# Softmax sums over all eight key blocks on GpSimd, the rotation's sums on VectorE, a part of the output division on ScalarE

## The chip, the cores and the metric

The kernel runs on one core of one Trainium2 chip. The metric is the device time of a run in microseconds (us). The kernel before was timed three times; a profile of one further execution was taken. In this text PE is TensorE, DVE is VectorE, ACT is ScalarE, POOL is GpSimd, and SP is the queue that issues every DMA of this kernel.

## The reference

The input x has 4 batches of 1024 rows of 128 numbers. Three layers follow one another, each added to x: a mixture of 8 experts with a soft routing (half its output is added), an attention with 16 heads, and the same mixture again. The attention is

```
h = layernorm(x) * ln_scale + ln_bias
c_q, c_kv = h @ w_down_q.T, h @ w_down_kv.T              # 64 latents each
q, k, v = (c_q @ w_up_q.T), (c_kv @ w_up_k.T), (c_kv @ w_up_v.T)   # 16 heads of 64
q, k = rope(q), rope(k)      # e*cos - o*sin and e*sin + o*cos for the even and odd elements
attn = softmax(q k^T / 8)    # 1024 keys for each query
out  = (attn @ v) @ w_out.T + residual
```

All data are 32-bit floats. In the layers around it the attention is added to x once more.

## The kernel before

**Stages.** The first mixture takes about the first 230 us (`ffn`), the attention stands from about 250 to 1525 us, and the second mixture (`ffn2`) ends the kernel. Preparation of later stages (layer norms, projections to the latents, routing weights) runs in small steps in the background of the stage before, as generators: `attn_pre` and `ffn_pre`.

**Units, slots and groups.** Heads are taken in pairs, of which one lies on partitions 0 to 63 and the other on 64 to 127. A unit U is half a head pair: 512 queries of two heads against all 1024 keys. There are 64 units, 16 for each batch. The keys of a unit are taken in 8 blocks of 128, and one block of one unit is a slot. Four slots make a group, so a unit lasts two groups; there are 128 groups. The attention's main loop runs over the groups.

**A slot.** `score` (L734) computes the transposed scores of 128 keys by 512 queries in four matmuls for each of the two heads (L746); the last of the four subtracts the row maxima. ACT takes the exponential from PSUM into the tile `p` (L750), 1024 wide for both heads; there are 8 buffers of `p`. `values` (L764) multiplies `p` by the latents of its keys into the PSUM bank `psc` (L769). It runs one group later. PSUM has 8 banks: five rotate among the scores (psS0 to psS3 and psX), two take the maxima (psA), one the values (psC).

**Maxima.** `passA` (L709) runs 15 slots ahead and computes the same scores the other way round, one matmul (L720) for each head into psA0 or psA1, of which VectorE takes the maximum (L721). Eight such pairs of matmul and maximum belong to each group, spread between its score matmuls.

**Softmax sums.** `accumulate` (L754) adds up the blocks of `p` on GpSimd into `acc` (L762), 1024 wide. The constant `DIRECT = 1` says how many of the 8 blocks are left out of it. So GpSimd makes six additions for a unit, of blocks 0 to 6, and block 7 stands by itself. At the end of the group that follows the unit's two, `den` (L773) sums over the 128 keys on PE with a matrix of ones (L781): eight matmul records over `p` of block 7, eight over `acc`. ACT copies the sums out (L783), and two small DMAs on SP turn them into `dT`, a column for each 128 queries (L787, L789). One group later `outp` (L792) multiplies the unit's values by the output weights (L802) into psX for one head and psS3 for the other, as `bankO` says. Its inner function `add` takes the reciprocal of `dT` (L809) and, for each of the two heads and four row blocks, multiplies by it and adds to the residual X (L813), 128 wide, on VectorE.

**Rotation.** `rope` (L602) works in stages for one half of a head group, in attention every second (even) group. "fetch" reads latents, "mm" gives six matmuls (L624) to the group, even elements into psX and odd ones into psS3. "o" and "e" multiply each by two tables, 1024 wide, on VectorE into the SBUF tile `rt` (L631). "sum" adds the two halves of `rt` on GpSimd into the tile `eo` (L634), 1024 wide. A group later ACT rounds `eo` to a high part (L639, "hi0" and "hi1") and GpSimd computes the low part (L647, "lo"); the stages "dhi" and "dlo" store them by DMA. The first nine rotations run before the attention loop through `attn_first`, with the stages "o", "e" and "sum"; 55 run inside it.

**Order.** Every engine runs its instructions in the order in which this program gives them, and each SP DMA waits in that queue as well. In a group the loop gives: the score matmuls of both heads with the maxima between them, then matmuls of `outp` (odd groups) or of the rotation (even groups); one step of the preparation; `den` (even groups); the rotation's VectorE and GpSimd work; `add` of `outp` (odd groups); the casts; and the values of the group before, with another preparation step between them. `step(most, vector)` picks a generator whose next step is of a kind up to `most`: OTHER, VECTOR (VectorE work) or PE (matmuls or transposes and what reads them); with `vector` false, VECTOR steps are left out. Another `step(OTHER)` stands in the middle of the group's rows. The variables `hurry` and `late` steer these calls.

Of the kernel before, what the change touches and what calls it, by code (L numbers as in the profile page):

```python
# [10 lines left out]
F32 = mybir.dt.float32  # L11
F32R = mybir.dt.float32r
AF = mybir.ActivationFunctionType
ALU = mybir.AluOpType
# [4 lines left out]
B, S, D = 4, 1024, 128  # L19
# [3 lines left out]
TPB = S // 128  # L23
# [4 lines left out]
AHEAD = 15  # L28
NSLOT = B * 128
NGRP = NSLOT // 4  # L30
DIRECT = 1
PBUFS = 8
MAXIMA = ((3, 8, 13), (0, 5, 10))
OTHER, VECTOR, PE, NEVER = 0, 1, 2, 3
NROPE = 9
# [6 lines left out]
class Kernel:  # L42
# [559 lines left out]
    def rope(self, n, stage):  # L602


        nc, P = self.nc, self.prep
        w = self.rope_of.setdefault(n, {})
        b, m = divmod(n, 16)
        g, qk, h = m // 4, m // 2 % 2, m % 2
        scr = (self.k_scr if qk else self.q_scr)[b][g]
        cs = slice(512 * h, 512 * h + 512)  # L610

        if stage == "fetch":
            assert (b, h) in self.latents
            w["C"] = P.tile([128, 2, 512], F32R, name="C_l", bufs=2)
            for r in (0, 64):
                self.dma(out=w["C"][r:r + 64], in_=self.c_scr[b][h][64 - 64 * qk:128 - 64 * qk])
        elif stage == "mm":
            ps = w["ps"] = self.rope_banks
            hi, lo = w["C"][:, 0, :], w["C"][:, 1, :]

            def mm(k, eo):
                wt, c = ((self.wup1, hi), (self.wup1, lo), (self.wup2, hi))[k]
                r64 = slice(64 * eo, 64 * eo + 64)
                nc.tensor.matmul(ps[eo], wt[r64, qk * 4 + g, :], c[r64, :], start=k == 0, stop=k == 2)  # L624

            for eo in range(2):
                self.halves[eo] += [lambda k=k, eo=eo: mm(k, eo) for k in range(3)]
        elif stage in ("o", "e"):
            k = "eo".index(stage)
            ps = w["ps"][k].unsqueeze(1).to_broadcast([128, 2, 512])  # L630
            nc.vector.tensor_tensor(self.rt[:, 2 * k:2 * k + 2, :], ps, self.table[:, 1 - k:3 - k, cs], ALU.mult)  # L631
        elif stage == "sum":
            w["eo"] = P.tile([128, 2, 512], F32, name="eo", bufs=2)
            nc.gpsimd.tensor_tensor(w["eo"], self.rt[:, 0:2, :], self.rt[:, 2:4, :], ALU.add)  # L634
        elif stage in ("hi0", "hi1"):
            k = int(stage[2])
            if k == 0:
                w["hi"] = P.tile([128, 2, 512], F32R, name="hi_r")
            nc.scalar.copy(w["hi"][:, k, :], w["eo"][:, k, :])  # L639
        elif stage == "dhi":  # L640
            self.dma(out=scr[0:2, :, :, cs].rearrange("s h i t -> (h i) s t"), in_=w["hi"])
        elif stage in ("lo0", "lo1"):
            k = int(stage[2])
            eo = w["eo"][:, k, :]
            nc.gpsimd.tensor_tensor(eo.bitcast(F32R), eo, self.f(w["hi"][:, k, :]), ALU.subtract)  # L645
        elif stage == "lo":
            nc.gpsimd.tensor_tensor(w["eo"].bitcast(F32R), w["eo"], self.f(w["hi"]), ALU.subtract)  # L647
        elif stage == "dlo":
            self.dma(out=scr[2:4, :, :, cs].rearrange("s h i t -> (h i) s t"), in_=w["eo"])
            self.roped.add((b, g, qk, h))  # L650
            del self.rope_of[n]
# [140 lines left out]
    def outp(self, U, osb, dT):  # L792


        nc = self.nc
        P, half = divmod(U, 2)
        b, j = divmod(P, 8)
        po = self.bankO or self.psA

        def mm(i, hh):  # L800
            r = slice(64 * hh, 64 * hh + 64)
            nc.tensor.matmul(po[hh][:, i * 128:(i + 1) * 128], osb[r, i * 128:(i + 1) * 128], self.G[r, j, :], start=True, stop=True)  # L802

        for hh in range(2):
            self.halves[hh] += [lambda i=i, hh=hh: mm(i, hh) for i in range(4)]

        def add():
            rT = self.ms.tile([128, 8], F32, name="rT")
            nc.vector.reciprocal(rT, dT)  # L809
            for hh in (1, 0):  # L810
                for i in range(4):
                    x = self.X[:, b * TPB + 4 * half + i, :]
                    nc.vector.scalar_tensor_tensor(x, po[hh][:, i * 128:(i + 1) * 128], rT[:, 4 * hh + i:4 * hh + i + 1], x, ALU.mult, ALU.add)  # L813

        self.at(self.group, add)

    def run(self):
        nc, tc = self.nc, self.tc
# [104 lines left out]
        a, c, e = (NP - 3) % 3, (NP - 2) % 3, (NP - 1) % 3  # L923
# [15 lines left out]
        def step(most, vector=True):  # L939


            turns["next"] += 1
            found = []
            for i in range(2):
                k = 1 + (turns["next"] + i) % 2
                while streams[k] and streams[k][0] not in needs:
                    v = next(streams[k][0], self)
                    if v is self:
                        streams[k].pop(0)
                    else:  # L950
                        needs[streams[k][0]] = v or OTHER
                if streams[k] and need(k) <= most:
                    found.append(k)
            found = [k for k in found if vector or need(k) != VECTOR]
            if found:
                k = max(found, key=need)
                gen = streams[k][0]
                kind = need(k)
                v = next(gen, self)
                if v is self:  # L960
                    streams[k].pop(0)
                else:
                    needs[gen] = v or OTHER
                return kind
            return OTHER


        ROPE = {"mid": {2: "dhi"}, "side": {0: "mm"}, "end": {-1: "fetch", 0: "o e sum", 2: "dlo"}, "cast": {1: "hi0 hi1 lo"}}

        def rope(g, place):  # L970
            for d, stages in ROPE[place].items():
# [5 lines left out]
        for g in range(NGRP + 1):  # L977
            s0 = 4 * g
            self.group, self.slot = g, s0
            rope(g, "side")  # L980
            self.run_later(g, "side")

            def rows(hh):
                maxima = lambda i: self.passA(s0 + AHEAD + i, hh) if s0 + AHEAD + i < NSLOT else None
                for n in range(16):
                    if n in MAXIMA[hh]:
                        yield lambda n=n: maxima(MAXIMA[hh].index(n))
                    yield lambda n=n: self.score(s0 + n // 4, hh, n % 4) if g < NGRP else None  # L990
                if hh == 1:
                    yield lambda: maxima(3)
                yield from side[hh]
                if hh == 0:
                    yield lambda: maxima(3)

            side = self.halves
            for n, pair in enumerate(zip_longest(rows(0), rows(1))):
                for fn in pair:
                    if fn:  # L1000
                        fn()
                if n == 9:
                    rope(g, "mid")
                    self.run_later(g, "mid")
                    step(OTHER)
            self.halves = [[], []]

            b, i = divmod(s0, 128)
            if i == 8 and 1 <= b < B:
                streams[1].append(pre2(b - 1))  # L1010
            self.nrest = 0
            hurry = g < 16 or g >= NGRP - 8
            late = step(PE, hurry) == PE or g % 2 == 0 or hurry or g >= 88
            if g and g % 2 == 0:
                self.den(g // 2 - 1)
            rope(g, "end")
            self.run_later(g, "end")
            if g == 1 or (g < NGRP and g % 4 == 3):
                P = g // 4 + 3 if g > 1 else 2
                if P < NP:  # L1020
                    for n, fn in enumerate(self.loads(P)):
                        self.at(g + 1 + n // 8, fn, ("mid", "end")[n // 4 % 2])
                if P == NP + 1:
                    self.ffn_weights2(self.QT[a], self.KT[a], self.QT[c])
                    self.dma(out=xs[0], in_=self.x2_scr[0])

            rope(g, "cast")
            for s in range(s0 - 4, s0):
                if s >= 0:
                    self.values(s)  # L1030
                if s == s0 - 3:
                    step(VECTOR, late)
        for i in range(2):
            for k in range(2):
                for hl in range(2):
                    c = slice(512 * k, 512 * k + 512)
# [3 lines left out]
        with ExitStack() as ctx:  # L1040
# [5 lines left out]
            g = self.ffn_pre(self.prep, (6, 7), x_of, self.wts2[:, 3].rearrange("p e t -> p t e"), rows=3)  # L1046
# [65 lines left out]
```

## Time and profile before

| | us |
|---|---|
| median of 3 runs | 1679.14 |
| lowest, highest | 1677.74, 1685.03 |
| the profiled execution's own time | 1681.56 |
| its span, first to last instruction | 1679.8 |
| PE busy in the span | 1620.7 |
| GpSimd busy | 1467.3 |
| VectorE busy | 1272.5 |
| ScalarE busy | 932.9 |
| mean granted TensorE clock | 0.990 |

The page of a profile gives the busy time and its share of the span for each engine, and then the span in 40 slices of 42 us with the busy share of each in tenths. A group line reads: source line, engine, operation, tile written <- tiles read, shapes, count, then the busy time in us and the mean duration in ns, then how long the engine stood idle just before these instructions and who ended that. Two figures of one instruction kind must be kept apart: its duration, and the distance from one start to the next when several follow one another, which is often shorter, since the end of one overlaps the start of the next. A timeline line gives start, length, engine, line and count. Matmuls overlap, so PE's busy time is that of the union.

### The profile page before, as it was taken

The page shows a single profiled execution, that of the slowest core. Times are in us where ns is not written, and L with a number is a line of the kernel's source. Part 1 is how long each engine was busy: PE and PEld are TensorE (multiplying, and loading weights), DVE is VectorE, ACT ScalarE, POOL GpSimd, SP SyncE. Part 2 cuts the span into 40 slices and gives each one's busy share as a digit, 9 for nine tenths or more (in the row PEclk, how much of TensorE's full clock was granted, in tenths as well). Part 3 has the DMA queues.
Part 4 walks back from the last instruction along what each step waited for, and adds up shares of the span by engine and source line. Part 5 has one row for each costly group of instructions (what it writes and reads, how often), then busy time and mean ns, then how long its engine had stood idle before and what let it go on. Part 6 is the DMA issues. An engine that isn't in the chain of part 4 may idle for free.

```text
span 1679.8 us, 31615 instructions
## 1 busy us (share of the span) xinstructions
PE 1620.7 (96%) x11412; PEld 1055.3 (63%) x11412; DVE 1272.5 (76%) x2456; ACT 932.9 (56%) x1964; POOL 1467.3 (87%) x821
## 2 busy tenths in 40 slices
PE   7897989999999999999999999999999999999998
PEld 5786665566656566665656566665666655656776
DVE  5674667878878778787778888887887877835887
ACT  4674565655565555655555555555555554555554
POOL 5658779999999999998999999999999987786676
PEclk9998999999999999999999999999999999999999
DMA  7024647555555555555555555555556632034443
GB/s 222 1 62 131 172 126 168 142 140 145 128 127 140 135 143 141 127 139 139 127 139 127 139 143 137 127 140 139 142 131 146 137 93 64 2 90 128 141 136 99
DMA packets 241148, 212.30 MB, mean 126 GB/s; under 512 B 157664, under 2 KB 170592, under 8 KB 240224
## 3 DMA queue, kind: packets, MB, share of 16 engines
q1 hardware_dynamic: 240992, 210.28, 49.5%
q8 instruction: 90, 1.47, 0.4%
q14 instruction: 66, 0.54, 0.1%
HBM read 130.39 MB, written 79.82 MB: 125 GB/s over the span
## 4 chain that ended last, share of the span: by engine, by line
PE 75%; POOL 7%; DVE 4%; ACT 3%; issue 3%; DMA 1%; SPq 1%; DVEq 0%; POOLq 0%; ACTq 0%
PE psc L769 23%; PE ps_s L746 22%; PE ps_a L720 6%; POOL acc L762 4%; PE ps_s L781 3%; PE ps_s L498 3%; PE psx L746 3%; PE ps_s L418 3%; PE psx L453 2%; PE psx L802 2%; PE psx L624 1%; PE ps_s L802 1%; ACT p L750 1%; PE psc L389 1%; SPq L51 1%
## 5 line engine op out<-in xcount | busy, mean ns | idle before, releaser
L721 DVE TENSOR_REDUCE m<-ps_a 128x1 f32<-128x512 f32 x1024 | 685.2, 690 | 231.9 <-PE ps_a L720 190.0
L762 POOL TENSOR_TENSOR acc<-acc,p 128x1024 f32<-128x1024 f32 x320 | 761.1, 2378 | 33.2 <-ACT p L750 13.7
L750 ACT ACTIVATE p<-ps_s 128x512 f32<-128x512 f32 x896 | 478.5, 602 | 308.4 <-PE ps_s L746 298.0
L746 PE MATMUL ps_s<-QT,KT 64*128 64x512 f32 x2688 | 551.3, 398 | 1.4 <-DVE rt L631 0.6
L769 PE MATMUL psc<-p,ckn 128*64 128x512 f32 x2048 | 467.7, 598 | 0.0
L746 PEld LDWEIGHTS ps_s<-QT,KT 64*128 64x128 f32 x2688 | 352.2, 185 | 138.1 <-issue 93.3
L720 PE MATMUL ps_a<-KT,QT 64*128 64x512 f32 x1024 | 420.3, 421 | 11.1 <-DVE m L721 8.3
L769 PEld LDWEIGHTS psc<-p,ckn 128*64 128x64 f32 x2048 | 135.6, 136 | 255.8 <-issue 249.8
L746 PE MATMUL ps_s<-maxr,one_row 64*128 64x512 f32 x896 | 238.4, 392 | 0.0
L720 PEld LDWEIGHTS ps_a<-KT,QT 64*128 64x128 f32 x1024 | 185.2, 185 | 43.2 <-DVE m L721 17.6
L762 POOL TENSOR_TENSOR acc<-p 128x1024 f32<-128x1024 f32 x64 | 152.9, 2388 | 42.4 <-ACT p L750 42.2
L634 POOL TENSOR_TENSOR eo<-rt 128x1024 f32<-128x1024 f32 x64 | 153.9, 2405 | 2.0 <-DMA qs<-eo 1.9
L771 ACT COPY osb<-psc 128x512 f32<-128x512 f32 x64 | 37.6, 588 | 195.5 <-PE psc L769 195.5
L647 POOL TENSOR_TENSOR eo<-eo,hi_r 128x1024 fp32r<-128x1024 f32 x55 | 132.0, 2401 | 0.0
L746 PEld LDWEIGHTS ps_s<-maxr,one_row 64*128 64x128 f32 x896 | 123.2, 185 | 13.3
L402 POOL TENSOR_TENSOR X<-X,dtmp 128x512 f32<-128x512 f32 x54 | 69.2, 1282 | 57.6 <-ACT dtmp L401 49.4
L746 PE MATMUL psx<-QT,KT 64*128 64x512 f32 x384 | 111.0, 394 | 0.0
L506 POOL TENSOR_TENSOR p<-eo,p 128x512 fp32r<-128x512 f32 x42 | 64.0, 1531 | 35.0 <-ACT p L505 27.4
L639 ACT CAST hi_r<-eo 128x512 fp32r<-128x512 f32 x128 | 73.9, 626 | 23.4 <-POOL eo L645 21.6
L813 DVE SCALAR_TENSOR_TENSOR X<-ps_s,rT,X 128x128 f32<-128x128 f32 x252 | 71.1, 344 | 15.4 <-PE ps_s L802 8.2
L750 ACT ACTIVATE p<-psx 128x512 f32<-128x512 f32 x128 | 77.0, 602 | 4.9 <-ACT p L750 1.8
L746 PEld LDWEIGHTS psx<-QT,KT 64*128 64x128 f32 x384 | 71.2, 186 | 7.3
(219 smaller groups left out, 2355.6 us busy)
## 6 DMA issues: line engine op xcount, KB each, us to landing
C_l<-cs SPq DMA_DIRECT2D x128, 256.0 KB
QT<-qs SPq DMA_DIRECT2D x256, 128.0 KB
KT<-ks SPq DMA_DIRECT2D x256, 128.0 KB
qs<-hi_r SPq DMA_DIRECT2D x32, 512.0 KB
qs<-eo SPq DMA_DIRECT2D x32, 512.0 KB
ks<-hi_r SPq DMA_DIRECT2D x32, 512.0 KB
ks<-eo SPq DMA_DIRECT2D x32, 512.0 KB
rt<-wt SPq DMA_DIRECT2D x52, 256.0 KB
```

What stands on the lines that cost most here:

```text
L402: nc.gpsimd.tensor_tensor(X[:, t:t + 4, :], X[:, t:t + 4, :], tmp, ALU.add)
L506: (nc.gpsimd if m < N - 1 else nc.vector).tensor_tensor(sh[:, 1, :], hp, self.f(sh[:, 0, :]), ALU.subtract)
L634: nc.gpsimd.tensor_tensor(w["eo"], self.rt[:, 0:2, :], self.rt[:, 2:4, :], ALU.add)
L639: nc.scalar.copy(w["hi"][:, k, :], w["eo"][:, k, :])
L647: nc.gpsimd.tensor_tensor(w["eo"].bitcast(F32R), w["eo"], self.f(w["hi"]), ALU.subtract)
L720: nc.tensor.matmul(self.psA[hh], self.QT[P % 3][r, 0, q0:q0 + 128], self.KT[P % 3][r, 0, kk * 512:kk * 512 + 512], start=True, stop=True)
L721: nc.vector.tensor_reduce(m[0][:, hh, qb, kk:kk + 1], self.psA[hh], AX.X, ALU.max)
L746: nc.tensor.matmul(ps, w, x, start=k == 0, stop=k == 3)
L750: nc.scalar.activation(self.p_of[s][:, hh, :], ps, AF.Exp, scale=0.125)
L762: nc.gpsimd.tensor_tensor(acc, self.p_of[s - 1] if c == 1 else acc, self.p_of[s], ALU.add)
L769: nc.tensor.matmul(self.psC[64 * hh:64 * hh + 64, :], self.ckn[b % 2][:, c, :], self.p_of[s][:, hh, :], start=c == 0, stop=c == 7)
L813: nc.vector.scalar_tensor_tensor(x, po[hh][:, i * 128:(i + 1) * 128], rT[:, 4 * hh + i:4 * hh + i + 1], x, ALU.mult, ALU.add)
```

## The change

`DIRECT` becomes 0: GpSimd adds block 7 to `acc` too, as a seventh addition, and `den` multiplies only `acc` by the ones.

The rotation inside attention gets one stage, "vector", for "o e sum". VectorE multiplies the even elements by two tables into `rt`, as "e" did; it multiplies the odd elements by each of the two tables into the PSUM banks of the even and the odd elements, in place; and it adds each bank to a half of `rt`, into `eo`. The stages "o", "e" and "sum" stay for the nine first rotations.

In `add`, ScalarE multiplies the first head's four blocks by the reciprocals, in their PSUM bank. VectorE multiplies and adds the second head's four blocks as before, and then adds the whole first bank, 512 wide, to X.

The loop's preparation steps are steered by a new variable, `free`, true in groups below 16, in odd groups, and from group 112 on. Where it is false, only steps of the kind OTHER are taken.

```diff
-DIRECT = 1
+DIRECT = 0
...
+        elif stage == "vector":
+            w["eo"] = P.tile([128, 2, 512], F32, name="eo", bufs=2)
+            (even, odd), rt = w["ps"], self.rt
+            nc.vector.tensor_tensor(rt[:, 0:2, :], even.unsqueeze(1).to_broadcast([128, 2, 512]), self.table[:, 1:3, cs], ALU.mult)
+            nc.vector.tensor_tensor(even, odd, self.table[:, 0, cs], ALU.mult)
+            nc.vector.tensor_tensor(odd, odd, self.table[:, 1, cs], ALU.mult)
+            nc.vector.tensor_tensor(w["eo"][:, 1, :], odd, rt[:, 1, :], ALU.add)
+            nc.vector.tensor_tensor(w["eo"][:, 0, :], even, rt[:, 0, :], ALU.add)
...
-            for hh in (1, 0):
-                for i in range(4):
-                    x = self.X[:, b * TPB + 4 * half + i, :]
-                    nc.vector.scalar_tensor_tensor(x, po[hh][:, i * 128:(i + 1) * 128], rT[:, 4 * hh + i:4 * hh + i + 1], x, ALU.mult, ALU.add)
+            t0 = b * TPB + 4 * half
+            for i in range(4):
+                c = slice(i * 128, (i + 1) * 128)
+                nc.scalar.activation(po[0][:, c], po[0][:, c], AF.Identity, scale=rT[:, i:i + 1])
+            for i in range(4):
+                x = self.X[:, t0 + i, :]
+                nc.vector.scalar_tensor_tensor(x, po[1][:, i * 128:(i + 1) * 128], rT[:, 4 + i:5 + i], x, ALU.mult, ALU.add)
+            x = self.X[:, t0:t0 + 4, :]
+            nc.vector.tensor_tensor(x, po[0].rearrange("p (t d) -> p t d", t=4), x, ALU.add)
...
-        ROPE = {"mid": {2: "dhi"}, "side": {0: "mm"}, "end": {-1: "fetch", 0: "o e sum", 2: "dlo"}, "cast": {1: "hi0 hi1 lo"}}
+        ROPE = {"mid": {2: "dhi"}, "side": {0: "mm"}, "end": {-1: "fetch", 0: "vector", 2: "dlo"}, "cast": {1: "hi0 hi1 lo"}}
...
-            hurry = g < 16 or g >= NGRP - 8
-            late = step(PE, hurry) == PE or g % 2 == 0 or hurry or g >= 88
+            free = g < 16 or g % 2 == 1 or g >= 2 * (16 * B - NROPE) + 2
+            step(PE if free else OTHER, free)
...
-                    step(VECTOR, late)
+                    step(VECTOR, free)
```

## The prediction

> **What bounds the kernel now.** I read the page first: busy shares, then the 40 slices.
>
> ```profile
> PE 1620.7 (96%) x11412; PEld 1055.3 (63%) x11412; DVE 1272.5 (76%) x2456; ACT 932.9 (56%) x1964; POOL 1467.3 (87%) x821
> PE   7897989999999999999999999999999999999998
> POOL 5658779999999999998999999999999987786676
> ```
>
> PE stands at 9 from slice 7 to the last but one, and POOL at 8 or 9 from slice 7 to 33: two engines are nearly full in the attention stage (about 250 to 1525 us). So I asked for the busy time of its middle, 345 to 1345 us, and for POOL's waits there.
>
> ```profile
> core 0: us, PE busy (x) PEld busy (x) DVE busy (x) ACT busy (x) POOL busy (x), PEclk, DMA share, GB/s
> 345.00:1345.00 1000.00, 989.58 (x7528) 606.40 (x7526) 805.68 (x1545) 557.90 (x1117) 962.57 (x437) 1.00 0.57 137
> ```
>
> ```profile
> POOL acc L762 <- ACT p L750: 20.3, 26, 3.5
> ```
>
> PE is busy for 989.6 of 1000 us at a granted clock of 1.00; POOL for 962.6, and it waits only 20.3 us. The rest, some 17 us, are gaps of about 0.04 us between its 437 instructions. **PE sets the pace, but POOL has 2% left.** That is the number on which this case turns.
>
> Next one unit U (half a head pair, two groups) in the timeline. PE first, at the end of an even group:
>
> ```profile
> 1032.52 0.64 PE L781 MATMUL ps_s<-p,ones 128*32 128x256 f32 x8
> 1032.98 0.61 PE L781 MATMUL ps_s<-acc,ones 128*32 128x256 f32 x8
> 1033.52 3.65 PE L769 MATMUL psc<-p,ckn 128*64 128x512 f32 x16
> ```
>
> The denominators' two parts start 0.46 us apart. The unit before started at 1013.11, so a clean unit lasts 19.41 us. From 363.5 to 1332.2 us there are 48 unit periods, 20.18 us each: the mean has preparation and late DMAs in it. GpSimd in the same unit:
>
> ```profile
> 1018.25 2.41 POOL L634 TENSOR_TENSOR eo<-rt 128x1024 f32<-128x1024 f32 x1
> 1020.61 7.29 POOL L762 TENSOR_TENSOR acc<-acc,p 128x1024 f32<-128x1024 f32 x3
> 1027.86 2.40 POOL L647 TENSOR_TENSOR eo<-eo,hi_r 128x1024 fp32r<-128x1024 f32 x1
> 1030.65 2.40 POOL L762 TENSOR_TENSOR acc<-p 128x1024 f32<-128x1024 f32 x1 [0.39 <-ACT p L750]
> 1033.13 4.83 POOL L762 TENSOR_TENSOR acc<-acc,p 128x1024 f32<-128x1024 f32 x2
> ```
>
> From 1018.25 to 1037.92 it rests 0.39 us: its unit's work is 19.67 - 0.39 = about 19.25 us, against PE's 19.41. VectorE at the end of the even group:
>
> ```profile
> 1031.95 1.34 DVE L721 TENSOR_REDUCE m<-ps_a 128x1 f32<-128x512 f32 x2 [0.26 <-PE ps_a L720]
> 1033.21 1.21 DVE L631 TENSOR_TENSOR rt<-ps_s,table 128x1024 f32<-128x1024 f32 x1
> 1034.35 1.21 DVE L631 TENSOR_TENSOR rt<-psx,table 128x1024 f32<-128x1024 f32 x1
> ...
> 1037.67 4.12 DVE L721 TENSOR_REDUCE m<-ps_a 128x1 f32<-128x512 f32 x6 [1.73 <-PE ps_a L720]
> ```
>
> The rotation's two products take 33.21 to 35.5; the next group's maxima come at 37.67 when PE delivers them, and from there VectorE (0.66 us a maximum) keeps step with PE's 0.7 us.
>
> **The change, part by part.**
>
> *Denominator on PE.* Half of L781 goes: one part of 0.46 us in each of 64 units, 29 us of PE work; 0.46 x 49.5 (1000/20.18) = **22.8 us** in the middle, 4.1 in the last nine units.
>
> *Sums on POOL.* A unit gets one more L762 (2.38 us) and, in the 55 units whose rotation runs inside attention, loses one L634 (2.405). In the middle that is zero: POOL's floor stays at 962.6 + 17 = **980 us**. It can win at most the 20.3 us of its waits. PE's floor becomes 989.6 - 22.8 = 967. So POOL becomes the bound: a clean unit goes from 19.41 to about 19.25, not 18.95, and only units with preparation on PE get the whole 0.46. The order moves too: 4 adds and the L647 now lie in the odd group, 3 adds in the even one. The den matmul (L781, even group) waits for the eighth block: four adds from about 1020.2 end at 1029.9, against den at 1032.5, a margin of 2.6 us where the sixth add had 32.5 - 27.9 = 4.6. Behind den in PE's queue are the values matmuls, and then the next scores; POOL has 9.6 us of work in hand by then, so it doesn't starve. Of its 20.3 us some 6 to 8 will stay idle around late DMAs (one dT is 6.26 us late in the chain at 775). Gain in the middle: 20 - 7 = **about 13 us**. Before 345 us the chain already runs through POOL's adds; nothing there.
>
> [...] The row says 2.38; I use it. [...]
>
> *The rotation on VectorE.* Removed: two L631 of 1.14 us start to start. Added: one of them, two multiplications PSUM to PSUM and two sums PSUM + SBUF to SBUF, 512 wide. Rows near these:
>
> ```profile
> L631 DVE TENSOR_TENSOR rt<-psx,table 128x1024 f32<-128x1024 f32 x57 | 69.3, 1216 | 0.0
> L401 ACT ACTIVATE dtmp<-psc,wts 128x128 f32<-128x128 f32 x116 | 33.1, 370 | 20.8 <-PE psc L389 20.8
> L512 DVE TENSOR_TENSOR eo<-eo,rt 128x512 f32<-128x512 f32 x35 | 37.4, 1069 | 1.2
> L511 DVE TENSOR_TENSOR eo<-eo,ps_s 128x512 f32<-128x512 f32 x21 | 14.3, 682 | 13.8 <-ACT eo L501 12.0 <-PE ps_s L498 1.6
> ```
>
> L511 (one operand in PSUM) is 0.68 us, L512 (both in SBUF, beside GpSimd) 1.07. [...] All the new ones have one operand in PSUM: 0.65 each, start to start. Stage: 1.14 + 4 x 0.65 = **3.75 us** (before 2.28). By the L512 row the two sums would make it 4.6. A write into PSUM isn't in the trace: I bound it by the 0.6 of a fast neighbour and by 0.95. The stage ends at 33.21 + 3.75 = 36.96; PE, 0.46 us earlier, finishes the first maximum's matmul at 37.05. It fits with nothing over. Two banks hold the maxima and PE's third waits for the first reduce, so about 0.4 us more is free, and beyond **4.3 us** PE stalls. The banks themselves (psS3, psX) are needed only at the second slot of the next group, after 1038. The eo buffer it writes was last read by a DMA issued some 19 us before: no wait.
>
> *Output projection.* VectorE: eight L813 (0.26 us apart, 2.1) become four and one 512-wide sum, 1.04 + 0.65; ScalarE gets 4 x 0.27 = 1.1 us (four L401 in a row take 1.12 to 1.15). It starts when rT is there, beside VectorE's four, so the sum ends where the eighth L813 did: **0**. ScalarE's cover is the 3.9 us that it rests after the hi casts; the casts move back about 2 us, and so do their DMA on SP's queue and the L647, which POOL reaches only at 1029.9. Without that cover it would be 1.1 us a unit. When dT is late (14 times, 26.5 us), ScalarE now waits too; PE was stopped there before, by the same banks.
>
> *The order of preparation.* PE and VectorE steps of the streams go to odd groups alone. Middle VectorE preparation is about 23 us; an odd group has some 0.7 us of room, so a dozen of the long steps (L349 takes 1.42) may cost PE 0.5 each, 6 us, most of it inside PE's new 13 us slack. I count 2.
>
> *End of attention.* Here POOL is late already:
>
> ```profile
> 1521.81 0.64 PE L781 MATMUL ps_s<-acc,ones 128*32 128x256 f32 x8 [1.08 <-POOL acc L762]
> ```
>
> One more add (2.4) for each of the last two units goes ahead of this den, behind which the last values stand: about 3.5 us lost, against 8 x 0.46 = 3.7 won. **Net 0 to 1.**
>
> Sum: 13 - 2 + 1 = **12 us**. The profiled span is 1679.8, its run 1681.6, the median 1679.1, so span to median is -0.7: 1679.8 - 12 - 0.7 = **1667 us**.
>
> **The rivals.**
>
> A. *POOL paces* (the above): 1660 to 1674, chance 0.50.
>
> B. *PE's whole saving comes through*: POOL's waits vanish, 20 in the middle and 4 at the end: 1655. For it: POOL's queue smooths over units. Against: its idle time must go to zero. 0.15.
>
> C. *Nothing moves*: with two engines at 98% and 2.6 us of margin, den waits for POOL as often as it won. About 1679. For it: before 345 us the page's chain is POOL's already, at PE 93.3 of 95. 0.15.
>
> D. *VectorE becomes the bound in the even group, slower.* If dependent PSUM instructions take 0.95 instead of 0.65, the stage is 4.95 us, 0.65 over the 4.3 at the first maximum; x 54 = 35 us, less PE's 23: with POOL idle for it too, about 1692. It decides from a stage of about 4.8 us (0.5 x 54 = 27). For it: the trace has no PSUM-to-PSUM instruction, and the maxima leave VectorE no room to recover within a group. Against: L511. 0.20.
>
> **How the numbers follow.** A 0.5% bound (8.4 us) is about what a measurement of this kernel tells from no change. A: 0.42 faster, 0.08 same; B: 0.15 faster; C: 0.02, 0.11, 0.02; D: 0.03 same, 0.17 slower. Faster 0.59, same 0.22, slower 0.19. The range reaches from just under B to most of D: 1654 to 1692; A's own is 1660 to 1674.
>
> **What would show it.** Right: L781 half as many and 0.46 us a unit; POOL in the middle at 98 to 99%, with den matmuls now waiting for L762; clean units at 19.2 to 19.3; the five VectorE instructions in 3.7 to 3.9 us. Wrong: clean units at 18.95 with POOL not waiting (B); maxima matmuls waiting for VectorE at the start of odd groups (D); ScalarE's scaling delaying the exponentials; the last den waiting over 5 us.

## The result and the profile after

The changed kernel takes 1744.9 us (median of 4 runs, 1741.6 to 1748.8) against 1679.3 us before (now 4 runs). The ratio is 1.0392, with a 95% interval from 1.0375 to 1.0409: it is 65 us slower, where 12 us less were forecast and 1692 us was the upper end of the range.

The page of the changed kernel, busy time by engine and then two groups from its list (idle time just before them, and who ended it, at the end of the line):

```profile
PE 1630.7 (94%) x10900; PEld 1063.2 (61%) x10900; DVE 1325.3 (76%) x2429; ACT 1023.1 (59%) x2220; POOL 1494.0 (86%) x830
...
L824 ACT ACTIVATE psx<-psx,rT 128x128 f32<-128x128 f32 x252 | 86.3, 343 | 161.8 <-DVE rT L819 137.2
...
L819 DVE RECIPROCAL rT<-dT 128x8 f32<-128x8 f32 x64 | 12.5, 195 | 100.5 <-DMA dT<-d 100.5
```

PE has 512 matmul records fewer and is busy 10 us longer. Outside its busy time it stands 1742.7 - 1630.7 = 112 us, where it stood 59: 53 us more. The two together are the 63 us between the spans. That PE is busy longer with less work goes in the main with its clock: the mean granted clock fell from 0.990 to 0.975, some 26 us of the span. The new ScalarE instruction (L824) waited 137 us for the reciprocals, and those waited 100.5 us for the transfer of dT; before it was 40.9.

The middle of the attention in the table by stretches, with the same columns as before:

```profile
345.00:1345.00 1000.00, 953.19 (x6824) 587.12 (x6824) 816.85 (x1470) 600.30 (x1255) 919.29 (x415) 0.98 0.53 130
```

No engine is full any more: PE fell from 989.6 to 953 us of 1000, GpSimd from 962.6 to 919. A wait has become the bound. Who PE waits for in that stretch (total us, times, longest):

```profile
PE ps_a L730 <- DVE m L731: 29.0, 24, 2.3
PE ps_s L756 <- DVE X L827: 14.7, 12, 3.3
```

Before, these were 5.4 and 0.3 us:

```profile
PE ps_a L720 <- DVE m L721: 5.4, 5, 1.6
PE ps_s L746 <- DVE X L813: 0.3, 1, 0.3
```

L827 is the output projection's VectorE part, which holds the bank psS3 until dT is there. VectorE's own wait for dT in the stretch, and ScalarE's behind it, then VectorE's before:

```profile
DVE rT L819 <- DMA dT<-d: 66.1, 22, 5.0
ACT psx L824 <- DVE rT L819: 108.0, 39, 7.2
```

```profile
DVE rT L809 <- DMA dT<-d: 17.1, 12, 3.7
```

And what SP's queue itself waits for, after and then before:

```profile
SPq L51 <- ACT hi_r L649: 255.1, 44, 11.2
SPq L51 <- DMA d<-m: 108.1, 48, 4.2
```

```profile
SPq L51 <- ACT hi_r L639: 149.8, 35, 8.0
SPq L51 <- DMA d<-m: 70.7, 49, 3.5
```

The first of each pair is the wait for the rounded high part of the rotation (the casts, L649 in the changed kernel and L639 before), the second the maxima's own round trip. How these belong together is seen in one unit. First SP's queue, then VectorE and ScalarE:

```profile
996.29 0.37 SPq L51 DMA_DIRECT2D qs<-hi_r  x1
996.70 2.26 SPq L51 DMA_DIRECT2D QT<-qs  x4
999.06 0.37 SPq L51 DMA_DIRECT2D d<-m  x1
1002.55 0.57 SPq L51 DMA_DIRECT2D maxr<-d  x1
1003.21 3.21 SPq L797 DMA_DIRECT2D d<-dsb  x1
...
1011.14 0.42 SPq L799 DMA_DIRECT2D dT<-d  x1
...
1020.23 0.38 SPq L51 DMA_DIRECT2D qs<-hi_r  x1
```

```profile
1017.39 0.20 DVE L819 RECIPROCAL rT<-dT 128x8 f32<-128x8 f32 x1 [4.82 <-DMA dT<-d]
...
1017.69 1.47 ACT L824 ACTIVATE psx<-psx,rT 128x128 f32<-128x128 f32 x4 [4.44 <-DVE rT L819]
1019.08 1.12 ACT L649 CAST hi_r<-eo 128x512 fp32r<-128x512 f32 x2
```

dT lands at 1017.4, 4.8 us late. ScalarE has stood since 1013.2 at L824, because that waits for the reciprocal. Behind it in ScalarE's queue are the casts, so they run at 1019.1. The store of the high part, `qs<-hi_r`, waits for them at the head of SP's queue and goes at 1020.2. Behind it stand the maxima's transfers, the softmax sums' store and the next dT. It is a **loop through two queues**: late dT, late casts, late store, late dT.

Where the time goes by unit: the start of each unit's L781/L791 record over `acc` in one profile, less the same unit's in the profile before (us).

| unit | changed kernel | VectorE divides (e1) |
|---|---|---|
| 0 | +2.5 | +0.2 |
| 12 | +12.7 | -0.4 |
| 24 | +21.5 | -1.2 |
| 36 | +32.3 | -10.5 |
| 48 | +42.7 | -10.4 |
| 62 | +55.8 | -10.3 |

The loss grows as long as there are rotations: at unit 54 it is 56.3 us. The last casts of a rotation run at 1402 us; from there to 1538 us no dT is late, and nothing more is lost up to unit 62. The profile of e1 is that of its fastest run; its median lies 9 us higher.

### The profile page after: what moved, and what is told of

The parts are those of the page before. It is cut to its first block, busy times and chain, and to the rows that moved or that the text cites. A ratio compares the mean times of both kernels' runs of the same rounds, so it can differ in the third digit from the quotient of the medians.

```text
span 1742.7 us, 30985 instructions
## 1 busy us (share of the span) xinstructions
PE 1630.7 (94%) x10900; PEld 1063.2 (61%) x10900; DVE 1325.3 (76%) x2429; ACT 1023.1 (59%) x2220; POOL 1494.0 (86%) x830
## 4 chain that ended last, share of the span: by engine, by line
PE 47%; DMA 6%; SPq 6%; POOL 6%; DVE 6%; ACT 4%; issue 3%; POOLq 0%; ACTq 0%; DVEq 0%
PE ps_s L756 15%; PE psc L779 15%; DMA dT<-d 5%; PE ps_a L730 5%; SPq L51 4%; POOL acc L772 4%; PE ps_s L498 2%; ACT psx L824 2%; PE psx L756 2%; DVE m L731 2%; PE psx L453 2%; PE ps_s L791 2%; SPq L797 2%; PE psx L812 1%; PE psx L624 1%
## 5 line engine op out<-in xcount | busy, mean ns | idle before, releaser
L772 POOL TENSOR_TENSOR acc<-acc,p 128x1024 f32<-128x1024 f32 x384 | 914.6, 2382 | 77.7 <-ACT p L760 51.6
L756 PE MATMUL ps_s<-QT,KT 64*128 64x512 f32 x2688 | 581.9, 408 | 23.6 <-DVE X L827 19.6
L730 PE MATMUL ps_a<-KT,QT 64*128 64x512 f32 x1024 | 433.9, 434 | 39.3 <-DVE m L731 37.1
L756 PEld LDWEIGHTS ps_s<-QT,KT 64*128 64x128 f32 x2688 | 363.5, 190 | 167.9 <-issue 70.6
L756 PE MATMUL ps_s<-maxr,one_row 64*128 64x512 f32 x896 | 252.6, 400 | 0.0
L730 PEld LDWEIGHTS ps_a<-KT,QT 64*128 64x128 f32 x1024 | 190.5, 190 | 79.7 <-DVE m L731 54.9
L824 ACT ACTIVATE psx<-psx,rT 128x128 f32<-128x128 f32 x252 | 86.3, 343 | 161.8 <-DVE rT L819 137.2
L781 ACT COPY osb<-psc 128x512 f32<-128x512 f32 x64 | 37.6, 588 | 194.1 <-PE psc L779 194.1
L756 PEld LDWEIGHTS ps_s<-maxr,one_row 64*128 64x128 f32 x896 | 130.5, 190 | 13.2
L756 PE MATMUL psx<-QT,KT 64*128 64x512 f32 x384 | 117.5, 414 | 0.0
L819 DVE RECIPROCAL rT<-dT 128x8 f32<-128x8 f32 x64 | 12.5, 195 | 100.5 <-DMA dT<-d 100.5
L649 ACT CAST hi_r<-eo 128x512 fp32r<-128x512 f32 x128 | 73.1, 615 | 21.7 <-POOL eo L655 21.7
L827 DVE SCALAR_TENSOR_TENSOR X<-ps_s,rT,X 128x128 f32<-128x128 f32 x252 | 70.9, 344 | 14.1 <-PE ps_s L812 7.4
```

The costliest lines, as they stand in the source:

```text
L730: nc.tensor.matmul(self.psA[hh], self.QT[P % 3][r, 0, q0:q0 + 128], self.KT[P % 3][r, 0, kk * 512:kk * 512 + 512], start=True, stop=True)
L756: nc.tensor.matmul(ps, w, x, start=k == 0, stop=k == 3)
L772: nc.gpsimd.tensor_tensor(acc, self.p_of[s - 1] if c == 1 else acc, self.p_of[s], ALU.add)
L824: nc.scalar.activation(po[0][:, c], po[0][:, c], AF.Identity, scale=rT[:, i:i + 1])
L827: nc.vector.scalar_tensor_tensor(x, po[1][:, i * 128:(i + 1) * 128], rT[:, 4 + i:5 + i], x, ALU.mult, ALU.add)
```

## The experiments

Theory L is this loop, which begins where ScalarE's scaling stands ahead of the casts. Theory P says that preparation crowded into odd groups stops PE; theory G blames GpSimd's eighth block.

**e1: VectorE divides both heads again.**

```diff
-                nc.scalar.activation(po[0][:, c], po[0][:, c], AF.Identity, scale=rT[:, i:i + 1])
...
-            nc.vector.tensor_tensor(x, po[0].rearrange("p (t d) -> p t d", t=4), x, ALU.add)
+            for hh in (1, 0):
...
+                    nc.vector.scalar_tensor_tensor(x, po[hh][:, i * 128:(i + 1) * 128], rT[:, 4 * hh + i:4 * hh + i + 1], x, ALU.mult, ALU.add)
```

> The changed kernel, but VectorE divides both heads as before (no ScalarE instruction in the output projection). Theory L (a loop through two queues: ScalarE's scaling waits for dT and stands ahead of the hi casts; the casts hold the store of the high part on SP's queue, behind which the maxima's and the next unit's dT transfers stand): the waits of VectorE for dT fall from 66 us to under 35 us between 345 and 1345 us, SP's wait for the hi casts from 255 to about 150 us, and the time to 1660-1685 us. Theory P (preparation crowded into odd groups stops PE there): 1720 us or more. Theory G (GpSimd's later sums, with the denominator waiting for the eighth): 1720 us or more.

Measured 1687.0 us (1677.7 to 1690.3), ratio 1.0038 [1.0019, 1.0056]. VectorE's waits for dT fell from 66.1 to 19.8 us, SP's for the casts from 255.1 to 139.5. The time is 2 us over the range that L gave; P and G, with 1720 or more, are out as the main cause.

**e2: the division alone, in the kernel before.**

```diff
-            for hh in (1, 0):
...
+                nc.scalar.activation(po[0][:, c], po[0][:, c], AF.Identity, scale=rT[:, i:i + 1])
...
+            nc.vector.tensor_tensor(x, po[0].rearrange("p (t d) -> p t d", t=4), x, ALU.add)
```

> The kernel before with ScalarE dividing one head, nothing else changed. Theory L: most of the 65 us, 1715-1745 us, with SP waiting over 220 us for the hi casts. Theories P and G: within 10 us of the kernel before, 1670-1690 us.

1731.2 us, ratio 1.0293 [1.0257, 1.0328]; SP waits 249.2 us for the casts. One part of the change, by itself, makes 51 us of the 65. The late casts also hold GpSimd here, which takes the low part from them:

```profile
POOL eo L647 <- ACT hi_r L639: 45.3, 23, 4.0
```

That is not the way the loss takes: in the same stretch no wait of PE for GpSimd is listed, and ScalarE's comes to 0.8 us.

**e3: the changed kernel with the old preparation steps.**

```diff
-            free = g < 16 or g % 2 == 1 or g >= 2 * (16 * B - NROPE) + 2
-            step(PE if free else OTHER, free)
+            hurry = g < 16 or g >= NGRP - 8
+            late = step(PE, hurry) == PE or g % 2 == 0 or hurry or g >= 88
...
-                    step(VECTOR, free)
+                    step(VECTOR, late)
```

> The changed kernel with the old rule for preparation steps (hurry and late). Theory L: 1730-1755 us, still slow. Theory P: 1670-1695 us. Theory G: about 1740 us.

1737.4 us, ratio 1.0352 [1.0309, 1.0394], which overlaps the changed kernel's interval. P is out here too.

**e4: casts ahead of the scaling.** The same instructions on every engine, one order turned.

```diff
+            rope(g, "cast")
             self.run_later(g, "end")
...
-            rope(g, "cast")
```

> The changed kernel with one order turned: in an odd group the hi casts are issued before ScalarE's scaling, not after it; the same work on every engine. Theory L: the casts no longer wait for dT, SP's wait for them falls to about 150 us, VectorE's for dT under 35 us, and the time to 1660-1690 us. If ScalarE's extra work itself, or the way from VectorE over ScalarE back to VectorE, is what costs, and not the casts: still over 1725 us. Theories P and G: about 1740 us.

1685.6 us, ratio 1.0030 [1.0013, 1.0047]. VectorE waits 23.5 us for dT. SP's waits before the store of the high part stand under two names here:

```profile
SPq L51 <- ACT hi_r L649: 83.5, 16, 7.6
SPq L51 <- ACT psx L824: 61.8, 17, 7.7
```

The second is the casts as well: the timeline has most of these stores start about 0.03 us after the cast's end, when the scaling behind it (L824) has only begun. Together they are 145.3 us, near the kernel before and the expected 150. ScalarE's work is all there; its place in the queue alone was worth 59 us.

**e5: all eight blocks on GpSimd, alone.**

```diff
-DIRECT = 1
+DIRECT = 0
```

> The kernel before with all eight blocks summed on GpSimd, and the rotation's sums still there too. If GpSimd's time is the ceiling of a unit, as the prediction had it, its 7 x 2.41 + 2.36 + 2.40 = 21.6 us and 0.46 of preparation replace a mean unit of 20.18 us in 55 units: 1760-1800 us. If GpSimd had slack and only PE's saving counted: 1650-1660 us.

1796.1 us, ratio 1.069 [1.0663, 1.0717]: near the upper end of what GpSimd's ceiling gives. In the middle GpSimd is busy, and PE waits, as follows (a line of the stretches and one of the waits):

```profile
345.00:1345.00 1000.00, 915.21 (x6499) 545.27 (x6497) 736.50 (x1406) 513.49 (x1023) 981.13 (x444) 0.96 0.51 125
```

```profile
PE ps_s L781 <- POOL acc L762: 76.0, 36, 5.5
```

981 us busy is GpSimd full here: no wait of it is listed in the stretch, the other 18.9 us are the gaps between its 444 instructions (about 0.04 us each), and the waits of 20 us that it had in the kernel before are used up.

**e6: the rotation's sums on VectorE, alone.** The stage "vector" is that of the change.

```diff
-        ROPE = {"mid": {2: "dhi"}, "side": {0: "mm"}, "end": {-1: "fetch", 0: "o e sum", 2: "dlo"}, "cast": {1: "hi0 hi1 lo"}}
+        ROPE = {"mid": {2: "dhi"}, "side": {0: "mm"}, "end": {-1: "fetch", 0: "vector", 2: "dlo"}, "cast": {1: "hi0 hi1 lo"}}
```

> The kernel before with the rotation's sums on VectorE and nothing else. If the five VectorE instructions fit between two groups' maxima (prediction): 1672-1688 us, with no more waits of the maxima's matmuls for VectorE than before. If the stage is too long (rival D): 1700 us or more.

1682.2 us, ratio 1.0015 [1.0003, 1.0028]. The maxima's matmuls wait 3.5 us for VectorE in the middle, 5.4 before. Rival D is out.

**e7: the changed kernel with an early load of dT.** The scaling stays ahead of the casts.

```diff
-        self.at(self.group + 1, lambda: nc.sync.dma_start(out=dT, in_=d1.rearrange("(h x) (y p) -> p (h x y)", x=2, p=128)), "mid")
+        nc.sync.dma_start(out=dT, in_=d1.rearrange("(h x) (y p) -> p (h x y)", x=2, p=128))
```

> The changed kernel, scaling still ahead of the casts, but the load of dT is issued on SP right behind the store of the sums, ahead of the next group's stores and loads. Theory L with late dT as the seed of the loop: dT is there when VectorE asks, waits for it fall under 15 us between 345 and 1345 us, SP's wait for the casts to under 200 us, and the time to 1665-1690 us. If the casts' place behind the scaling costs even with dT in time: over 1710 us.

1683.0 us, ratio 1.0017 [1.0005, 1.0028]. VectorE waits 5.5 us for dT, SP 130.3 for the casts. The loop opens at this end too: with dT in time, the scaling in front of the casts costs at most a few us.

**e8: three mends.** Casts first (as in e4), early dT (as in e7), and block 7 of the last two units left to PE:

```diff
-        elif c < 8 - DIRECT:
+        elif c < 8 - (U >= 62):
...
-        parts = [self.p_of[8 * U + c] for c in range(8 - DIRECT, 8)] + [self.acc_of[U]]
+        parts = [self.p_of[8 * U + c] for c in range(8 - (U >= 62), 8)] + [self.acc_of[U]]
```

> The changed kernel with the casts ahead of the scaling, the early load of dT, and block 7 of the last two units left to PE as before. Units of 19.3 us (GpSimd's pace) and a last denominator that waits 1 us for GpSimd, not 5.9: 1655-1672 us if the prediction's 12 us were lost to these three alone; 1675 us or more if something else in the change costs.

1676.2 us, ratio 0.9969 [0.9958, 0.9981]: faster than both kernels, but in the second range (1675 us or more). So the 12 us were not lost to these three alone: the rest of the change doesn't win what was forecast. The last unit loses nothing here (the last two denominators are both 5.7 us ahead of the kernel before).

**e9: the changed kernel with the store of the high part behind the softmax sums' store on SP.**

```diff
-        ROPE = {"mid": {2: "dhi"}, "side": {0: "mm"}, "end": {-1: "fetch", 0: "vector", 2: "dlo"}, "cast": {1: "hi0 hi1 lo"}}
+        ROPE = {"mid": {}, "side": {0: "mm"}, "end": {-1: "fetch", 0: "vector", 2: "dhi dlo"}, "cast": {1: "hi0 hi1 lo"}}
```

> The changed kernel, scaling ahead of the casts as it is, but the store of the rotation's high part is issued on SP behind the store of the softmax sums (group's end), not in the group's middle ahead of the maxima's and the sums' transfers. If the loop closes on SP's queue through this store (theory L): the maxima and the sums are no longer held, VectorE's waits for dT fall from 66 us to under 40 us between 345 and 1345 us, 1670-1700 us. If it closes elsewhere (dT late by itself, ScalarE's casts holding GpSimd): 1720 us or more.

1710.7 us, ratio 1.0164 [1.0146, 1.0182]: neither range. The maxima and the sums are no longer behind the store, and 34 of the 65 us are gone. But dT now has both 512 KB stores and eight loads ahead of it, and VectorE still waits 52.6 us. The store's place closes a part of the loop. How much of the rest is the 1 MB in front of dT and how much dT's own lateness isn't told apart by this run; e7 shows only that both go with an early load.

**e10: division alone, casts first**, in the kernel before (e2 with e4's order).

```diff
+            rope(g, "cast")
             self.run_later(g, "end")
...
-            rope(g, "cast")
```

> The kernel before with ScalarE dividing one head and the casts issued ahead of it. Theory L: the division itself costs next to nothing, 1675-1690 us, where the same division ahead of the casts took 1731 us. If the division's own way (VectorE to ScalarE and back) costs: 1700 us or more.

1681.8 us, ratio 0.9999 [0.9984, 1.0014]. In the kernel before, the division on ScalarE costs nothing and brings nothing once the casts go first. Against e2, the order alone is 49 us.

**e11: e8 with VectorE dividing both heads.**

```diff
-                nc.scalar.activation(po[0][:, c], po[0][:, c], AF.Identity, scale=rT[:, i:i + 1])
...
+                    nc.vector.scalar_tensor_tensor(x, po[hh][:, i * 128:(i + 1) * 128], rT[:, 4 * hh + i:4 * hh + i + 1], x, ALU.mult, ALU.add)
```

> The three mends (casts first, early dT, block 7 of the last two units to PE), but VectorE divides both heads. If ScalarE's share of the division is worth something once the order is right, this is slower than the 1676 us with it, 1680 us or more; if it is worth nothing: 1672-1679 us.

1671.6 us, ratio 0.9943 [0.9925, 0.9962]: the lowest median, with eight blocks and the rotation as in the change. It is 4.6 us under e8, in which ScalarE divides one head; the two intervals just overlap, so that part of the change won nothing here and may have cost a little.

**e12: the kernel before with the early load of dT**, the two lines of e7:

```diff
-        self.at(self.group + 1, lambda: nc.sync.dma_start(out=dT, in_=d1.rearrange("(h x) (y p) -> p (h x y)", x=2, p=128)), "mid")
+        nc.sync.dma_start(out=dT, in_=d1.rearrange("(h x) (y p) -> p (h x y)", x=2, p=128))
```

> The kernel before with the early load of dT and nothing else. If late dT already cost the kernel before (26.5 us of VectorE's waits): 1655-1674 us, and the mended kernel's 4 us come from the mend, not from the change. If it was covered there: 1676-1684 us.

1672.6 us, ratio 0.9940 [0.9925, 0.9955]. dT's lateness cost the kernel before 9 us. **And e11 and e12 are level**: their medians lie 1 us apart, and each interval reaches about 3 us to either side. Once dT is early, no run shows a gain from the change's eight blocks and rotation. The middle of e12 and of e11, by stretches, shows why. First e12:

```profile
345.00:1345.00 1000.00, 994.59 (x7604) 607.75 (x7602) 809.41 (x1559) 561.52 (x1126) 972.20 (x442) 1.00 0.56 138
```

Then e11:

```profile
345.00:1345.00 1000.00, 983.48 (x7230) 600.93 (x7226) 884.71 (x1712) 564.03 (x1131) 974.97 (x441) 1.00 0.55 138
```

And e11's waits there, of PE for GpSimd and of GpSimd:

```profile
PE ps_s L791 <- POOL acc L772: 9.9, 11, 3.2
...
POOL acc L772 <- ACT p L760: 1.1, 3, 0.5
```

GpSimd is as full in the one as in the other: 972 and 975 us. In e12 PE is full beside it (994.6). In e11 PE is busy 11 us less, and waits 9.9 us for GpSimd's sums. So nearly all that PE saves goes into waiting for GpSimd.

## Why the prediction was wrong, point by point

**The output projection** is the step that failed: "VectorE ... **0**. ScalarE's cover is the 3.9 us that it rests after the hi casts; the casts move back about 2 us, and so do their DMA on SP's queue". The new instructions took 0.34 us each and 1.47 for four, where 1.1 was assumed, and in the kernel before they are covered (e10). What was costed at nothing is a wait. The text said that ScalarE would now wait for a late dT, and stopped at PE's banks. It named the casts behind it, and their store on SP, but didn't ask what stands behind that store: the maxima and the next dT itself. Among its signs of being wrong stood "ScalarE's scaling delaying the exponentials", without a cost. And dT was already at the edge: the kernel before waited for it 12 times, 17.1 us, in the middle (the 26.5 us of the prediction have 8.7 of the end of the attention in them). Measured: 51 us for this part alone (e2), 49 of them its place in the queue (e2 against e10).

**The clock** was missing from the sum. PE's new 13 us of slack were taken to absorb stalls. But after stalls PE ran at half speed for a while (granted clock 0.50, rows at the end): the mean clock fell by 0.015, some 26 us of the span, beside 53 us more in which PE stood still. By this estimate each wait is paid nearly one and a half times. Against these 26 us stand about 29 us of matmuls saved, and yet PE is busy 10 us longer: some 13 us of that stay open.

**The denominator** was right: half the records, and clean units of e1 follow one another in 19.25 and 19.31 us (1025.88, 1045.13, 1064.44), where 19.25 was forecast and 19.41 measured before.

**GpSimd as the ceiling** was right (its unit's work comes to 19.28 us by the sum shown, not 19.25): e5 had the time that it gives, and in e1 GpSimd waits 1.3 us of 1000 while den waits for it. The forecast "20 - 7 = about 13 us" in the middle was too high by the sizes: between units 6 and 54, e11 wins 13.3 us on the kernel before, but e12, without the change, wins 8.9 there. By these single profiles the change itself is worth 4.4, and 3.5 of these it has lost before unit 6 (e11 stands 1.9 us behind the kernel before there, e12 1.6 ahead), where the prediction had nothing; why it loses there stays open. About half of GpSimd's 20.3 us of waits were there because dT was late: with the early load alone (e12) 10.4 are left.

**The rotation** was right in kind: the five instructions take 4.03 us from the first's start to the next maximum (1002.59 to 1006.62), where 3.75 were reckoned and 4.3 was the limit (the first maximum's matmul of the kernel before ends at 1037.61, so 37.15 with the 0.46 off, not 37.05):

```profile
1002.59 1.21 DVE L637 TENSOR_TENSOR rt<-psx,table 128x1024 f32<-128x1024 f32 x1
1003.90 0.70 DVE L638 TENSOR_TENSOR psx<-ps_s,table 128x512 f32<-128x512 f32 x1
1004.51 0.69 DVE L639 TENSOR_TENSOR ps_s<-ps_s,table 128x512 f32<-128x512 f32 x1
1005.29 0.69 DVE L640 TENSOR_TENSOR eo<-ps_s,rt 128x512 f32<-128x512 f32 x1
1005.90 0.68 DVE L641 TENSOR_TENSOR eo<-psx,rt 128x512 f32<-128x512 f32 x1
1006.62 4.12 DVE L731 TENSOR_REDUCE m<-ps_a 128x1 f32<-128x512 f32 x6
```

The starts lie 1.31, 0.61, 0.78, 0.61 and 0.72 us apart. The two writes into PSUM took 0.70 and 0.69 us (the same over all 55 stages), where the row with one PSUM operand says 0.68; the sum that needs the product just ahead of it starts 0.78 after it, 0.17 later than the others. The 55 stages agree: their median is 3.99 us to the end of the fifth instruction. That the row of L511 (0.68) and not that of L512 (1.07) would hold for the two sums was the author's estimate; over the 55 stages they took 0.69 and 0.68. No row of the kernel before shows the 0.95 us from start to start that rival D took for dependent instructions; over the 55 stages the distance from the second product to the sum that needs it is 0.78 in the median (1.13 to 1.15 in three of them), and the distances before and after it are 0.61.

**The preparation steps** (2 us) made no difference that e3 can show.

**The end of attention** was too small: 3.5 us lost were forecast. In e1 the last denominator stands 10.3 us ahead at unit 62 and 6.0 at unit 63, and the values behind it run slow:

```profile
1515.82 1.08 PE L791 MATMUL ps_s<-acc,ones 128*32 128x256 f32 x8 [5.91 <-POOL acc L772]
1516.83 4.65 PE L779 MATMUL psc<-p,ckn 128*64 128x512 f32 x16
```

4.3 us by the wait and 1.0 by the clock (4.65 against 3.65, at a mean granted clock of 0.72 from 1515.8 to 1521.4), so 5.3.

None of the rivals named this way. D, the one on the slower side, took VectorE in even groups for the danger; the waits of the maxima's matmuls that did come stand behind dT.

## What to carry to other kernels

When an engine gets a new instruction that waits for a transfer, follow everything behind it in its queue down to the next queue, and from there until you meet the transfer again: if you do, a wait feeds itself. Put work that is ready ahead of work that waits for a DMA: here that order alone was worth 59 us (e4). And before counting an idle share as room for new work, ask why it is idle: here it was idle because of the transfer, and a load issued earlier in its queue won about 9 us with no other change.

## What the runs showed of the hardware

The granted clock fell soon after PE was only partly idle. Six microseconds of the changed kernel, one row each (first the stretch, its length and PE's busy time; the granted clock is third from the right):

```profile
1017.00:1018.00 1.00, 0.60 (x5) 0.17 (x1) 0.48 (x3) 0.31 (x1) 1.00 (x1) 1.00 1.05 229
1018.00:1019.00 1.00, 0.09 (x2) 0.09 (x2) 0.85 (x4) 0.90 (x4) 0.96 (x1) 1.00 0.59 131
1019.00:1020.00 1.00, 0.41 (x2) 0.09 (x2) 0.81 (x2) 1.00 (x3) 0.00 (x0) 1.00 0.08 29
1020.00:1021.00 1.00, 0.47 (x4) 0.42 (x5) 1.00 (x2) 1.00 (x3) 0.72 (x1) 1.00 0.02 8
1021.00:1022.00 1.00, 1.00 (x10) 0.93 (x8) 0.97 (x4) 0.87 (x3) 1.00 (x1) 0.71 0.87 332
1022.00:1023.00 1.00, 1.00 (x8) 1.00 (x7) 0.47 (x1) 0.52 (x1) 1.00 (x2) 0.50 0.58 197
```

PE's longest single wait here is 1.31 us. Between 1017 and 1021 us it was busy for 1.57 of 4 us, and after it had begun to work again the clock went to 0.50 and stayed low until 1025. The middle of this profile has ten such falls, 41 us at half speed in all, where the kernel before has one of 3.4 us. In the 4 us ahead of each of the ten PE was busy for 17 to 62%, and its longest stand up to then was 2.4 us (3.3 in all). How much idle time it takes for a fall isn't shown.
